# Layer 0 of a four-layer graph kernel: a whole last row tile, one broadcast on VectorE, later weight loads and a new order list

## The chip, the core and the metric

The kernel runs on one core of a Trainium2 chip. The metric is the device time of one execution in microseconds (us), the median of several runs. The core has five engines that the profile names PE (TensorE, the matrix engine; PEld is its weight load), DVE (VectorE), ACT (ScalarE), POOL (GpSimd) and SP (SyncE, which here only issues DMAs). Sixteen DMA engines move data between HBM and the on-chip memory.

## The reference

Node features `x` (2708 x 128) pass through four layers of message passing over a sparse weighted adjacency matrix `adj` (2708 x 2708, about 2.4% of it not zero). After each layer the result is added to `x` and normalized. Only layer 0 is touched by the change:

```
s = x @ msg_w[:, :128].T;  d = x @ msg_w[:, 128:].T
messages[i, j] = gelu(s[i] + d[j] + msg_b)          # 128 numbers for each pair
aggregated[i] = sum over j of adj[i, j] * messages[i, j]
h = gelu(concat(x, aggregated) @ upd_w.T + upd_b) + x
x = layernorm(x + layernorm(h))
...  # layers 1 to 3
```

## The kernel before

**Tiles.** A gelu for every pair would be 2708 x 2708 x 128 of them. The kernel uses that most pairs have weight zero. The rows i are cut into `LT` = 22 row tiles of `LR` = 125 rows, each in `NC` = 5 groups of `RG` = 25; the columns j into `NB` = 22 blocks of `JB` = 124. Within one block each row rarely has more than `CAP` = 5 neighbours. So each neighbour gets a rank within its block, and a slot (row, rank) in one of 5 x 25 partitions of a group. The matrices `S` (one-hot, 16-bit) pick for each slot the row of `d` and the weight; a product with `same` adds `s`.

**One block, on the engines.** PE `begin` (L1099) puts `s` into one of three PSUM slots `sl`; PE `pick` (L1107) adds the picked `d` and puts the weights beside it; ACT (L145) takes the gelu into one of six buffers `g`; DVE `weigh` (L1124) makes the small matrix `W`; PE `add_up` (L1115) multiplies `W` by `g` and sums into `acc`. After 22 blocks ACT copies `acc` out (L1120, `out`): that is the hand-over of a row tile. `turn` (L1049 to L1052) and `close` (L1056) turn the sum into a column range of `aggT`.

**What each row tile needs beforehand.** For each of three thirds of the columns: the load of `at` (L953, L956, the adjacency transposed, issued on SP), a `mask` on DVE (L879), ranks by a triangular matmul on PE (L886), a cast on ACT (L889), five `S` on DVE (L909), the weights in two 16-bit parts, `hi` on ACT (L902) and `lo` on DVE (L904). The untransposed rows `ar` come by six loads (L962). They serve the neighbours with a rank past `CAP`: DVE keeps their weights (`past`, L928), finds the largest (L936) and their columns (L982); POOL gathers the rows of `d` by index (L993) onto rows of `s` (started by a load on SP, L985); ACT and DVE weigh and sum them into `extra`. All this is done while the row tile before is in its blocks.

**The last row tile.** 21 x 125 = 2625, so 83 rows are left. Before, the last tile loads 83 rows and columns (`self.r = 83`), and DVE clears each `at` first (L877).

**The start.** `turn_x` transposes `x`; `prepare(n)`, n = 0 to 5, computes four blocks of `d` and four tiles of `s` and of `u` (the x part of the update), splits them into 16-bit `hi` and `lo` (ACT L831, DVE L840, L837), spreads `d` over the five groups (`spread_over`, on POOL, L798) and stores four tables to HBM from SP (L803, L806).

**The order.** The order of instructions on each engine is not written by hand. `Order.add` takes steps with an engine, an assumed cost, a due time (in units of blocks) and what they read and write; `Order.run` plays them through in Python at build time and emits them in the order in which they start. At each moment an engine takes the ready step with the smallest due time; PE adds `STAY` to the due time of a step that is of another kind than the one before:

```
s = min(can, key=lambda s: (s.due[0] + self.STAY * (s.kind != kinds.get(e, s.kind)), s.due[1]))
```

The kinds on PE are `"s"` (begin), `"all"` (pick, ranks, turn) and `"sums"` (add_up). The result is a fixed list; on the chip each engine goes through its own list in order and waits where data are not there yet.

**Weights of later layers.** `weight`, `column`, `across` and `side_by_side` load a weight at the first call. Before, the first calls are in layers 1 to 3, and the program's scheduler issues these DMAs early: they lie between 9 and 48 us in the profile.

Of the kernel before, what the change touches and what calls it, by code (L numbers as in the profile page):

```python
# [23 lines left out]
P = 128  # L24
# [56 lines left out]
class Order:  # L81
# [6 lines left out]

    LATENCY, TURN, STAY = 0.12, 0.1, 3.0

# [65 lines left out]
class Plan:  # L156
# [7 lines left out]
    LOAD, LATENCY = 1.28, 0.2  # L164
# [84 lines left out]
def gnn_stack(ctx: ExitStack, tc: tile.TileContext, t, out: bass.AP):  # L249
    nc = tc.nc  # L250
    N, D = t["x"].shape
# [69 lines left out]
    class Values:  # L321
# [33 lines left out]
        def add(self, a, b):  # L355
            return self.tt(a, b, ALU.add)
# [250 lines left out]
    NB = 22  # L607
# [21 lines left out]
    with ExitStack() as l0:  # L629
# [10 lines left out]
        with ExitStack() as msg:  # L640
# [79 lines left out]
            def columns_of(sl, a, b):  # L720
# [6 lines left out]
            order = Order()  # L727
            DUE = {"load": -69.5, "load_s": 34, "load_row": -9, "start_far": 204.5, "rank": -21, "rank_row": -18.5,
                   "begin": -0.8, "pick": -0.5, "add_up": 3.5, "turn": 34, "out": 41, "cast": -20, "a_hi": 7,
                   "gelu": -7.5, "far_weigh": 96, "close": 72.5, "far_gelu": 101.5, "weigh": -60.5, "largest": -8.5,  # L730
                   "index": 7.5, "mask": -12, "far_sum": -14.5, "past": -59.5, "max": -3, "a_lo": 1, "S": 1,
                   "fetch": 176}
            add = order.add
# [21 lines left out]
            def prepare(n):  # L755

                b0, b1 = 4 * n, min(4 * n + 4, NB)
                a0, a1 = 4 * n, min(4 * n + 4, NT)
                due = 4 * n - 40
                kd, ks = 2 * n % 3, (2 * n + 1) % 3  # L760
# [36 lines left out]
                def spread_over(v):  # L797
                    nc.gpsimd.tensor_copy(v[:, :, 1:, :], v[:, :, 0:1, :].to_broadcast([JB, b1 - b0, NC - 1, D]))  # L798

# [5 lines left out]
                def store(tab, v):  # L805
                    nc.sync.dma_start(out=tab[a0 * P:a1 * P, :].rearrange("(n p) d -> p n d", p=P), in_=v)  # L806
# [18 lines left out]
                if N < a1 * P:  # L825
# [16 lines left out]
                    reads=[("g", gd), ("hi", n)], writes=[("lo", n)])  # L842
                add("POOL", 2.2, lambda: spread_over(lo), due + 1, reads=[("lo", n)], writes=[("lo", n, 1)])
                add("SP", 0.1, lambda: store(s_tab, s), due + 1, reads=[("far", gf)], writes=[("s_tab", n)], lag=4.0)
                add("SP", 0.2, store_d, due + 1, reads=[("g", gd)], writes=[("d_tab", n)], lag=4.0)
                add("SP", 0.2, store_parts, due + 1, reads=[("parts", gf), ("parts", gf, 1), ("far", gf)],
                    writes=[("sq_tab", n)], lag=4.0)
                add("PE", 1.0, u_products, due + 12, reads=x_in, writes=["acc"], lag=0.2)
                add("DVE", 0.7, u_out, due + 12, reads=["acc"], writes=[("g", gu)])
                add("SP", 0.1, lambda: store(u_tab, u), due + 12, reads=[("g", gu)], writes=[("u_tab", n)], lag=4.0)  # L850

            class Rows:


                def __init__(self, t):
                    self.t, self.r0 = t, t * LR
                    self.r = min(P, N - self.r0)
                    self.pieces = range(self.r0 // BANK, min(self.r0 + P - 1, N - 1) // BANK + 1)
                    self.agg, self.s3, self.v = agg, s3_all[t % 2], v_all[:, t, :]
                    self.extra, self.cand = extra_all[t % 2], cand_all[t % 2]  # L860

                def add(self):
                    t = self.t
                    first = t * NB
                    add("SP", 0.4, self.load_s, first + DUE["load_s"], reads=[("sq_tab", n) for n in self.pieces],
                        writes=[("s3", t % 2)], lag=4.0)
                    for h, (b0, b1) in enumerate(thirds):
                        self.add_third(h, first + b0, b1 - b0)
                    self.add_far(first)

                def add_third(self, h, due, n):
# [7 lines left out]
                    add("DVE", 0.63 * share, lambda: nc.vector.tensor_scalar(  # L879
# [16 lines left out]
                    for k in range(2):  # L896
# [3 lines left out]
                    hi, lo = (v[:, b0:b1, :, D:] for v in dA)  # L900
                    source = at[:, :n, :LR].rearrange("p b (c i) -> p b c i", c=NC)
                    add("ACT", 0.97 * share, lambda: nc.scalar.activation(hi, source, AF.Copy, scale=A_SCALE), due + DUE["a_hi"],  # L902
# [3 lines left out]
                        reads=[k_at, ("a_hi", h)], writes=[("a_lo", h)])  # L906
                    ranks = rk[:, :n, :LR].rearrange("p b (c i) -> p b c i", c=NC)
                    for k in range(CAP):
# [4 lines left out]
                def add_rows(self, m, mask, k_mask, due):  # L913
# [5 lines left out]
                    one, share = ("misc", t, m, "rows"), n / PB  # L919
                    add("SP", 0.1, lambda: self.load_row(m, ar), due + DUE["load_row"], writes=[k_ar], lag=5.0)  # L920

# [18 lines left out]
                def load_s(self):  # L940
                    for q in range(2):
                        src = sq_tab[q, self.r0:self.r0 + LR, :].rearrange("(c i) d -> i c d", c=NC)
                        for k, (a, e) in enumerate(spans(0, NC, 3)):
                            p = k * HALF + q * RG
                            nc.sync.dma_start(out=self.s3[p:p + RG, :e - a, :D], in_=src[:, a:e, :])

                def load(self, h, at):
                    r0, r = self.r0, self.r
                    b0, b1 = thirds[h]
                    full = min(b1, NFB)  # L950
                    src = adjT[b0 * JB:full * JB, r0:r0 + r].rearrange("(b p) i -> p b i", p=JB)
                    for p0, p1 in even(JB):
                        nc.sync.dma_start(out=at[p0:p1, :full - b0, :r], in_=src[p0:p1])  # L953
                    if full < b1:
                        for p0, p1 in even(N - NFB * JB):
                            nc.sync.dma_start(out=at[p0:p1, full - b0, :r],  # L956
                                              in_=adjT[NFB * JB + p0:NFB * JB + p1, r0:r0 + r])

                def load_row(self, m, ar):
                    b1 = min((m + 1) * PB, NB)  # L960
                    n_in = min(b1 * JB, N) - m * PB * JB
                    nc.sync.dma_start(out=ar.rearrange("p b j -> p (b j)")[:self.r, :n_in],  # L962
                                      in_=adj[self.r0:self.r0 + self.r, m * PB * JB:m * PB * JB + n_in])

                def add_far(self, first):
# [11 lines left out]
                    for n in range(NOV):  # L977
# [6 lines left out]
                            reads=[("v", t, n), *o_keys], writes=[("ix", f)])  # L984
                        add("SP", 0.1, lambda far=far: nc.sync.dma_start(  # L985
                            out=far, in_=s_tab[self.r0:self.r0 + P, :][:, None, :].to_broadcast([P, 8, D])), due + DUE["start_far"],
# [52 lines left out]
                def add_turn(self, due):  # L1039
                    one = ("misc", self.t, "turn")  # L1040
                    add("PE", 0.85, self.turn, due + DUE["turn"], reads=[("extra", self.t % 2), "agg"], writes=[one],
                        lag=0.08, take="misc", kind="all")
                    add("ACT", 0.2, self.close, due + DUE["close"], reads=[one],
                        writes=[("xT", k) for k in range(len(spans(0, NT, 4)))], give=("misc", one, 1))
# [9 lines left out]
                def close(self):  # L1054
                    ps = misc.rearrange("p a b -> p (a b)")
                    nc.scalar.copy(aggT[:, self.r0:self.r0 + LR].rearrange("p (c i) -> p c i", c=NC),  # L1056
                                   ps[:, :32 * NC].rearrange("p (c i) -> p c i", c=NC)[:, :, :RG])
# [1045 lines left out]
```

## Time and profile before

| | us |
|---|---|
| median of 3 runs | 1827.45 (1826.45 to 1828.74) |
| the profiled execution | 1825.73 |
| its span, first to last instruction | 1824.0 |
| from the span's start to the first pick (L1107) | 62.9 |
| hand-over of row tile 0 | 101.8 |
| hand-over of row tile 21, the last | 800.3 |

| engine | busy us | share of the span |
|---|---|---|
| PE | 1548.3 | 85% |
| DVE | 1350.9 | 74% |
| ACT | 1070.6 | 59% |
| POOL | 595.0 | 33% |

In lines of the profile, the first number of a timeline row is the start from the span's beginning, the second the time it took; then follow engine (SPq is SP's queue, where the time is that of issuing), line, operation, and the output and input tiles with buffer numbers left out. A bracket tells how long the engine was idle before and what ended that. In rows of groups, the numbers behind the bar are the busy time, the mean time of one in ns, and the idle time before them. A row of waits gives engine, tile and line that waited, what it waited for, the sum, the number of times and the longest.

### The profile page before, as it was taken

What the parts mean: (1) busy time and instruction counts of PE and PEld (TensorE: products, weight loads), DVE (VectorE), ACT (ScalarE), POOL (GpSimd) and SP (SyncE); (2) the same over time, 40 slices, a digit from 0 to 9 for tenths busy, and PEclk for the clock granted to TensorE, in tenths of its full rate; (3) what the DMA queues carried; (4) which work ended last, traced back from release to release, by engine and by line L of the source; (5) the groups of instructions that cost most, each with busy time, mean ns of one, the idle gap of its engine ahead of it and who ended that gap; (6) DMA issues with size and microseconds to landing.
All of it is one profiled execution on the core that took longest, in us unless ns stands there. A gap on an engine that the chain in (4) does not pass through costs nothing.

```text
span 1824.0 us, 36369 instructions
## 1 busy us (share of the span) xinstructions
PE 1548.3 (85%) x14033; PEld 937.2 (51%) x14033; DVE 1350.9 (74%) x3129; ACT 1070.6 (59%) x1846; POOL 595.0 (33%) x389
## 2 busy tenths in 40 slices
PE   5799999999999999563999993678888895399995
PEld 4577777777777777452444442322222342144442
DVE  8799999999999999566788858658875873850004
ACT  3487787888878788453353434668877753421003
POOL 7287767677777776351000000000000000000000
PEclk8799999999999999886999996669987897599997
DMA  8677767667676765232244400314333555253431
GB/s 193 161 157 145 160 133 172 140 156 150 137 169 138 166 144 109 56 64 92 98 152 153 153 5 0 105 39 143 141 125 108 166 158 239 87 212 123 152 127 33
DMA packets 228558, 235.40 MB, mean 129 GB/s; under 512 B 28140, under 2 KB 213294, under 8 KB 221786
## 3 DMA queue, kind: packets, MB, share of 16 engines
q1 hardware_dynamic: 183670, 212.18, 37.3%
q0 software_dynamic: 44704, 20.80, 9.8%
q8 instruction: 112, 1.84, 0.4%
q14 instruction: 72, 0.59, 0.1%
HBM read 217.77 MB, written 15.15 MB: 128 GB/s over the span
## 4 chain that ended last, share of the span: by engine, by line
PE 38%; DVE 7%; ACT 6%; issue 1%; DMA 0%; SPq 0%; ACTq 0%; DVEq 0%
PE acc L2000 11%; PE lg L1388 6%; PE acc L1395 5%; PE accV L1728 5%; PE ps L1656 4%; PE accO L1732 2%; PE ps L1711 2%; DVE arena L1690 1%; ACT arena L1662 1%; PE ps L1657 1%; ACT arena L1683 1%; DVE arena L1714 1%; ACT x L455 1%; PE ps L523 1%; PE ps_w L1356 1%
## 5 line engine op out<-in xcount | busy, mean ns | idle before, releaser
L993 POOL DMA_INDIRECT far<-d_tab,ix x308 | 522.4, 1696 | 231.9 <-ACT agg L1120 50.0
L145 ACT ACTIVATE g<-sl 128x640 f32<-128x640 f32 x484 | 334.9, 708 | 150.4 <-PE sl L1107 102.9
L1107 PE MATMUL sl<-dA,S 124*128 124x153 f16 x4840 | 384.6, 232 | 1.3 <-DVE S L909 1.3
L1107 PEld LDWEIGHTS <-S 124*128 124x128 f16 x4840 | 326.4, 98 | 64.6 <-issue 59.6
L1099 PE MATMUL sl<-s,same 50*128 50x459 f16 (+1 forms) x968 | 145.6, 332 | 30.3 <-DVE W L1124 28.7
L1115 PE MATMUL acc<-g,W 128*32 128x128 f32 x4840 | 163.9, 277 | 0.1
L1124 DVE TENSOR_TENSOR W<-sl,own 128x125 f32<-128x125 f32 x484 | 129.0, 278 | 31.9 <-ACT g L145 31.4
L1389 ACT ACTIVATE w<-lg,row_L_gnn_gate_bias 128x512 f32<-128x512 f32 (+1 forms) x132 | 83.4, 636 | 108.2 <-PE lg L1388 107.0
L1115 PEld LDWEIGHTS acc<-g,W 128*32 128x32 f32 x4840 | 126.6, 110 | 22.0 <-issue 11.3
L1643 POOL TENSOR_TENSOR arena<-arena,off 128x128 f32<-128x128 f32 (+1 forms) x22 | 21.7, 986 | 351.5 <-DMA arena<-in_adjT 284.0
L909 DVE TENSOR_SCALAR S<-rk 124x1000 f16<-124x1000 bf16 (+1 forms) x330 | 124.5, 421 | 9.9 <-PE sl L1107 9.9
L982 DVE FIND_INDEX8 ix<-v,o 128x8 uint32<-128x2728 f32 x44 | 131.7, 2994 | 0.0
L1728 PE MATMUL accV<-arena,X 128*128 128x512 f32 (+4 forms) x264 | 124.8, 593 | 6.5 <-DVE arena L1694 6.5
L1388 PE MATMUL lg<-qT,mT 128*128 128x512 f32 (+2 forms) x264 | 121.2, 548 | 3.7 <-ACT w L1389 3.1
L1395 PE MATMUL acc<-w,both 128*128 128x512 f32 (+2 forms) x264 | 121.3, 547 | 0.0
L525 DVE TENSOR_TENSOR g<-ps,row_L_gnn_b 128x512 f32<-128x512 f32 (+2 forms) x14 | 7.9, 573 | 148.3 <-PE ps L523 148.3
L1656 PE MATMUL ps<-XT 128*128 128x512 f32 (+8 forms) x150 | 90.3, 691 | 32.1 <-ACT arena L1662 26.5
L2000 PE MATMUL acc<-at,x 128*128 128x512 f32 (+2 forms) x156 | 66.2, 575 | 48.5 <-ACT x L455 48.5
L1023 ACT ACTIVATE far<-far,v 128x128 f32<-128x128 f32 x308 | 105.2, 412 | 0.7
L1390 DVE TENSOR_TENSOR w<-w,at 128x512 f32<-128x512 f32 (+1 forms) x132 | 82.6, 626 | 27.1 <-ACT w L1389 27.0
L936 DVE MAX8 cand<-o 128x8 f32<-128x248 f32 x242 | 90.7, 406 | 0.0
L1099 PEld LDWEIGHTS <-same 50*128 50x128 f16 x968 | 43.6, 94 | 90.3 <-issue 68.0
(359 smaller groups left out, 2564.9 us busy)
## 6 DMA issues: line engine op xcount, KB each, us to landing
at<-in_adjT SPq DMA_DIRECT2D x42, 1354.0 KB
ar<-in_adj SPq DMA_DIRECT2D x105, 248.0 KB
far<-s_tab SPq DMA_DIRECT2D x44, 512.0 KB
at<-in_adjT SPq DMA_DIRECT2D x42, 448.0 KB
arena<-in_adjT SPq DMA_DIRECT2D x21, 704.0 KB
arena<-in_adjT SPq DMA_DIRECT2D x21, 650.0 KB
held<-in_adjT SPq DMA_DIRECT2D x7, 1354.0 KB
f_tab<-arena SPq DMA_DIRECT2D x10, 704.0 KB
```

Of the source, the lines that this page charges most:

```text
L145: s.emit()
L982: add("DVE", 3.0, lambda n=n, ix=ix: nc.vector.max_index(ix, v[:, n * 8:n * 8 + 8], o_all[:, :NB * JB]), due + DUE["index"], reads=[("v", ...
L993: nc.gpsimd.indirect_dma_start(out=far[:, k, :], out_offset=None, in_=d_tab[:, :], in_offset=bass.IndirectOffsetOnAxis(ap=ix[:, k:k + 1], ...
L1099: nc.tensor.matmul(columns_of(sl, 0, DA)[:, a:e, :], same[p], self.s3[p, :e - a, :], start=True, stop=False)
L1107: nc.tensor.matmul(columns_of(sl, 0, DA)[:, c, :], S_all[h][:, n, c, :], dA[q][:, b, c, :], start=False, stop=q == 1 and c in (2, NC - 1))
L1115: nc.tensor.matmul(acc_all[q:q + 32, k, :], W_all[W][:, c, :], g_all[g][:, c, :], start=b == 0 and k == 0, stop=ends)
L1124: nc.vector.tensor_tensor(W[:, :, :RG], columns_of(sl, D, DA), own[:, None, :].to_broadcast([P, NC, RG]), op=ALU.mult)
L1388: nc.tensor.matmul(lg, mT[:, j * P:j * P + r], qT[:, a:b], start=True, stop=True)
L1395: nc.tensor.matmul(acc[k], mrow[:rows[j], j, :], ws[j][:rows[j], a:b], start=j == 0, stop=j == NT - 1)
L1656: nc.tensor.matmul(ps, XT[:, self.js], XT[:, c], start=True, stop=False)
L1728: nc.tensor.matmul(Pair.acc[0][:, a:b], X[:self.r, self.j, :], self.w_[:, a:b], start=first, stop=last)
L2000: nc.tensor.matmul(acc[k], src[:rows[j], j, :], at[:rows[j], a:b], start=j == order[0], stop=j == order[-1])
```

## The change

- **The last row tile** is rows 2580 to 2707, whole 128 rows; its last 125 are used (`o = 3`, `used`). Rows 2583 to 2624 are computed a second time. The three clears of `at` go. The matrix `spread`, which puts `extra` in place in `turn`, is rewritten for the last tile by a DVE copy behind the turn of tile 20.
- **`spread_over`** runs on VectorE instead of GpSimd (twelve copies, all at the start).
- **Later layers' weights**: eleven steps load them from within layer 0's list, placed behind the first gather, with due times one row tile apart from the fifth on.
- **The list is redone**: `STAY` is 42 instead of 3, nearly all due times are new, and steps on SP have costs of 0.4 to 1.7 where they had 0.1 to 0.4.

```diff
-    LATENCY, TURN, STAY = 0.12, 0.1, 3.0
+    LATENCY, TURN, STAY = 0.12, 0.1, 42.0
...
-            DUE = {"load": -69.5, "load_s": 34, "load_row": -9, "start_far": 204.5, "rank": -21, "rank_row": -18.5,
-                   "begin": -0.8, "pick": -0.5, "add_up": 3.5, "turn": 34, "out": 41, "cast": -20, "a_hi": 7,
-                   "gelu": -7.5, "far_weigh": 96, "close": 72.5, "far_gelu": 101.5, "weigh": -60.5, "largest": -8.5,
-                   "index": 7.5, "mask": -12, "far_sum": -14.5, "past": -59.5, "max": -3, "a_lo": 1, "S": 1,
-                   "fetch": 176}
+            DUE = {"piece": 0, "spread": -10, "s_out": 23.5, "d_out": 37, "u": 25, "load": -125, "load_s": 94.5,
+                   "load_row": -58.5, "start_far": 206, "rank": -20, "rank_row": -18.5, "begin": -1.8, "pick": 0.5,
+                   "add_up": 3, "turn": 34.5, "out": 57.5, "cast": -58.5, "a_hi": 21, "gelu": -9.5, "far_weigh": 97.5,
+                   "close": 113.5, "far_gelu": 106, "weigh": -63.5, "largest": -8.5, "index": -35, "mask": -10,
+                   "far_sum": -34, "past": -77, "max": -4.5, "a_lo": -12, "S": 4, "fetch": 211}
...
-                    nc.gpsimd.tensor_copy(v[:, :, 1:, :], v[:, :, 0:1, :].to_broadcast([JB, b1 - b0, NC - 1, D]))
+                    nc.vector.tensor_copy(v[:, :, 1:, :], v[:, :, 0:1, :].to_broadcast([JB, b1 - b0, NC - 1, D]))
...
-                add("POOL", 2.2, lambda: spread_over(hi), due, reads=[("hi", n)], writes=[("hi", n, 1)])
+                add("DVE", 0.65, lambda: spread_over(hi), due + DUE["spread"], reads=[("hi", n)], writes=[("hi", n, 1)])
...
-                add("SP", 0.1, lambda: store(s_tab, s), due + 1, reads=[("far", gf)], writes=[("s_tab", n)], lag=4.0)
-                add("SP", 0.2, store_d, due + 1, reads=[("g", gd)], writes=[("d_tab", n)], lag=4.0)
+                add("SP", 0.45, lambda: store(s_tab, s), due + DUE["s_out"], reads=[("far", gf)], writes=[("s_tab", n)], lag=4.0)
+                add("SP", 0.9, store_d, due + DUE["d_out"], reads=[("g", gd)], writes=[("d_tab", n)], lag=4.0)
...
-                add("PE", 1.0, u_products, due + 12, reads=x_in, writes=["acc"], lag=0.2)
+                add("PE", 1.0, u_products, due + DUE["u"], reads=x_in, writes=["acc"], lag=0.2)
...
-                    self.t, self.r0 = t, t * LR
-                    self.r = min(P, N - self.r0)
+                    self.t, self.r0 = t, min(t * LR, N - P)
+                    self.o = P - LR if t == LT - 1 else 0
+                    self.used = slice(self.o, self.o + LR)
...
-                    if self.r < P:
-                        add("DVE", 0.9, lambda: nc.vector.memset(at, 0.0), due + DUE["load"], writes=[k_at])
-                    add("SP", 0.2, lambda: self.load(h, at), due + DUE["load"], writes=[k_at], lag=7.0)
+                    add("SP", 0.8, lambda: self.load(h, at), due + DUE["load"], writes=[k_at], lag=7.0)
...
-                nc.sync.dma_start(out=ar.rearrange("p b j -> p (b j)")[:self.r, :n_in],
-                                  in_=adj[self.r0:self.r0 + self.r, m * PB * JB:m * PB * JB + n_in])
+                nc.sync.dma_start(out=ar.rearrange("p b j -> p (b j)")[:, :n_in],
+                                  in_=adj[self.r0:self.r0 + P, m * PB * JB:m * PB * JB + n_in])
...
+            for n, (engine, load) in enumerate((
+                    ("SP", side_by_side), ("SP", lambda: weight("L1_gnn_W_q")), ("SP", lambda: weight("L1_gnn_W_k")),
+                    ("SP", lambda: weight("L1_gnn_W_upd", P)), ("SP", lambda: column("L1_gnn_b_msg")),
+                    ("SP", lambda: weight("L3_gnn_W")), ("POOL", lambda: across("L1_gnn_gate_bias")),
+                    ("POOL", lambda: across("L1_gnn_ln_gamma")), ("POOL", lambda: across("L1_gnn_ln_beta")),
+                    ("POOL", lambda: across("L2_gnn_att_b")), ("POOL", lambda: across("L3_gnn_b")))):
+                add(engine, 0.55, load, (5 + n) * NB, reads=[("far", 0, 0)])
...
+            add("DVE", 0.2, lambda: nc.vector.tensor_copy(
+                spread[:, :, :RG], ident[:, R[-1].used].rearrange("p (c i) -> p c i", c=NC)), (LT - 1) * NB + 10,
+                writes=["spread"])
```

More of the change, by code (lines that the diff above doesn't have):

```diff
@@ L758, in prepare @@
                 a0, a1 = 4 * n, min(4 * n + 4, NT)
-                due = 4 * n - 40
+                due = 4 * n - 40 + DUE["piece"]
                 kd, ks = 2 * n % 3, (2 * n + 1) % 3
@@ L842, in prepare @@
                     reads=[("g", gd), ("hi", n)], writes=[("lo", n)])
-                add("POOL", 2.2, lambda: spread_over(lo), due + 1, reads=[("lo", n)], writes=[("lo", n, 1)])
-                add("SP", 0.1, lambda: store(s_tab, s), due + 1, reads=[("far", gf)], writes=[("s_tab", n)], lag=4.0)
-                add("SP", 0.2, store_d, due + 1, reads=[("g", gd)], writes=[("d_tab", n)], lag=4.0)
-                add("SP", 0.2, store_parts, due + 1, reads=[("parts", gf), ("parts", gf, 1), ("far", gf)],
+                add("DVE", 0.65, lambda: spread_over(lo), due + 1 + DUE["spread"], reads=[("lo", n)], writes=[("lo", n, 1)])
+                add("SP", 0.45, lambda: store(s_tab, s), due + DUE["s_out"], reads=[("far", gf)], writes=[("s_tab", n)], lag=4.0)
+                add("SP", 0.9, store_d, due + DUE["d_out"], reads=[("g", gd)], writes=[("d_tab", n)], lag=4.0)
+                add("SP", 0.9, store_parts, due + 1, reads=[("parts", gf), ("parts", gf, 1), ("far", gf)],
                     writes=[("sq_tab", n)], lag=4.0)
-                add("PE", 1.0, u_products, due + 12, reads=x_in, writes=["acc"], lag=0.2)
-                add("DVE", 0.7, u_out, due + 12, reads=["acc"], writes=[("g", gu)])
-                add("SP", 0.1, lambda: store(u_tab, u), due + 12, reads=[("g", gu)], writes=[("u_tab", n)], lag=4.0)
+                add("PE", 1.0, u_products, due + DUE["u"], reads=x_in, writes=["acc"], lag=0.2)
+                add("DVE", 0.7, u_out, due + DUE["u"], reads=["acc"], writes=[("g", gu)])
+                add("SP", 0.45, lambda: store(u_tab, u), due + DUE["u"], reads=[("g", gu)], writes=[("u_tab", n)], lag=4.0)
             class Rows:
                 def __init__(self, t):
-                    self.t, self.r0 = t, t * LR
-                    self.r = min(P, N - self.r0)
+                    self.t, self.r0 = t, min(t * LR, N - P)
+                    self.o = P - LR if t == LT - 1 else 0
+                    self.used = slice(self.o, self.o + LR)
                     self.pieces = range(self.r0 // BANK, min(self.r0 + P - 1, N - 1) // BANK + 1)
@@ L864, in add @@
                     first = t * NB
-                    add("SP", 0.4, self.load_s, first + DUE["load_s"], reads=[("sq_tab", n) for n in self.pieces],
+                    add("SP", 1.7, self.load_s, first + DUE["load_s"], reads=[("sq_tab", n) for n in self.pieces],
                         writes=[("s3", t % 2)], lag=4.0)
@@ L900, in add_third @@
                     hi, lo = (v[:, b0:b1, :, D:] for v in dA)
-                    source = at[:, :n, :LR].rearrange("p b (c i) -> p b c i", c=NC)
+                    source = at[:, :n, self.used].rearrange("p b (c i) -> p b c i", c=NC)
                     add("ACT", 0.97 * share, lambda: nc.scalar.activation(hi, source, AF.Copy, scale=A_SCALE), due + DUE["a_hi"],
@@ L906, in add_third @@
                         reads=[k_at, ("a_hi", h)], writes=[("a_lo", h)])
-                    ranks = rk[:, :n, :LR].rearrange("p b (c i) -> p b c i", c=NC)
+                    ranks = rk[:, :n, self.used].rearrange("p b (c i) -> p b c i", c=NC)
                     for k in range(CAP):
@@ L919, in add_rows @@
                     one, share = ("misc", t, m, "rows"), n / PB
-                    add("SP", 0.1, lambda: self.load_row(m, ar), due + DUE["load_row"], writes=[k_ar], lag=5.0)
+                    add("SP", 0.4, lambda: self.load_row(m, ar), due + DUE["load_row"], writes=[k_ar], lag=5.0)
                     def rank():
@@ L941, in load_s @@
                     for q in range(2):
-                        src = sq_tab[q, self.r0:self.r0 + LR, :].rearrange("(c i) d -> i c d", c=NC)
+                        src = sq_tab[q, self.r0 + self.o:self.r0 + self.o + LR, :].rearrange("(c i) d -> i c d", c=NC)
                         for k, (a, e) in enumerate(spans(0, NC, 3)):
@@ L947, in load @@
                 def load(self, h, at):
-                    r0, r = self.r0, self.r
+                    r0, r = self.r0, P
                     b0, b1 = thirds[h]
@@ L984, in add_far @@
                             reads=[("v", t, n), *o_keys], writes=[("ix", f)])
-                        add("SP", 0.1, lambda far=far: nc.sync.dma_start(
+                        add("SP", 0.45, lambda far=far: nc.sync.dma_start(
                             out=far, in_=s_tab[self.r0:self.r0 + P, :][:, None, :].to_broadcast([P, 8, D])), due + DUE["start_far"],
@@ L1040, in add_turn @@
                     one = ("misc", self.t, "turn")
-                    add("PE", 0.85, self.turn, due + DUE["turn"], reads=[("extra", self.t % 2), "agg"], writes=[one],
+                    add("PE", 0.85, self.turn, due + DUE["turn"], reads=[("extra", self.t % 2), "agg", "spread"], writes=[one],
                         lag=0.08, take="misc", kind="all")
@@ L1055, in close @@
                     ps = misc.rearrange("p a b -> p (a b)")
-                    nc.scalar.copy(aggT[:, self.r0:self.r0 + LR].rearrange("p (c i) -> p c i", c=NC),
+                    nc.scalar.copy(aggT[:, self.r0 + self.o:self.r0 + self.o + LR].rearrange("p (c i) -> p c i", c=NC),
                                    ps[:, :32 * NC].rearrange("p (c i) -> p c i", c=NC)[:, :, :RG])
```

## The prediction

> **What bounds the kernel now.** I read the busy slices of the page first, then the times at which each row tile of layer 0 hands over its sum (ACT, L1120), then the windows around whatever breaks the rhythm, and in those the timeline, the waits and the DMA answer. Times are microseconds.
>
> ```profile
> PE   5799999999999999563999993678888895399995
> PEclk8799999999999999886999996669987897599997
> ```
>
> A slice is 45.6 us. PE is near full in slices 3 to 16, and there are two weak places in the part that the change touches: the start (slices 1 and 2) and slices 17 and 18.
>
> ```profile
> 687.14 0.19 ACT L1120 ACTIVATION_READ_ACCUMULATOR agg<-acc 128x1 f32 x1
> 719.43 0.19 ACT L1120 ACTIVATION_READ_ACCUMULATOR agg<-acc 128x1 f32 x1
> 771.88 0.20 ACT L1120 ACTIVATION_READ_ACCUMULATOR agg<-acc 128x1 f32 x1
> 800.34 0.19 ACT L1120 ACTIVATION_READ_ACCUMULATOR agg<-acc 128x1 f32 x1
> ```
>
> Tile 0 hands over at 101.8, and from tile 5 on the distance is 32.33 each time (687.14 to 719.43 is one). Tile 20 takes 52.45. So 52.45 - 32.33 = 20.1 us are lost once, in tile 20, which is when tile 21, the last, is fetched and ranked ahead.
>
> ```profile
> 101.80:739.30 637.50, 626.51 (x10140) 484.74 (x10138) 602.08 (x1526) 514.47 (x1025) 470.62 (x276) 1.00 0.69 147
> 739.30:756.00 16.70, 0.12 (x2) 0.10 (x1) 0.94 (x3) 1.45 (x2) 7.01 (x5) 0.64 0.33 77
> ```
>
> The columns are the stretch, its length, busy PE, PEld, DVE, ACT and POOL, the granted clock, the DMA share and GB/s. In the loop PE is 98% busy and DVE 94%. From 739.3 to 756.0 all of them stand.
>
> ```profile
> 731.48 8.76 SPq L985 DMA_DIRECT2D far<-s_tab  x1
> 740.35 3.19 SPq L962 DMA_DIRECT2D ar<-in_adj  x1
> 743.62 4.36 SPq L953 DMA_DIRECT2D at<-in_adjT  x2
> ...
> 755.07 0.56 DVE L879 TENSOR_SCALAR mask<-at 124x768 bf16<-124x768 f32 x1 [17.05 <-DMA at<-in_adjT]
> ...
> 755.88 0.54 PE L1099 MATMUL sl<-s,same 50*128 50x459 f16 x2 [16.61 <-DVE W L1124]
> ```
>
> DVE waits 17.05 us for the last third of the last tile's `at`; `weigh` is behind it on DVE, and PE waits for `weigh`. That load was issued only at 743.6, because SP sat 8.76 us in one issue and 3.19 in the next, where such an issue takes 0.33 to 1.5 in the tile before. The DMA answer for 732 to 752 says why:
>
> ```profile
> GB/s 148 302 326 292 124 150 38 20 19 24 59 125 36 24 28 24 19 44 269 355 335 93 20 22 19 20 19 19 32 180 206 24 28 61 88 28 66 70 61 41
> ...
> ar<-in_adj SPq DMA_DIRECT2D x1, 160.8 KB
> ```
>
> For long stretches only 19 to 24 GB/s move, while loads of 128 rows reach 250 to 330. 160.8 KB are 83 rows of 1984 B; there the busy share of the 16 DMA engines is under a tenth, which is about one engine's pace. The last tile's six `ar` loads are five of 160.8 KB and one of 73.9 KB, together 0.90 MB; at 20 GB/s that is 45 us, more than the 32.3 us of a tile, and SP's later loads queue behind them.
>
> **The change, part by part.** The sum is made against the profiled execution, 1825.73 us (span 1824.0); the median, 1827.45, is 1.7 above it.
>
> *Last tile of 128 rows: -19.5 us.* The `ar` loads become the shape of all other tiles (248 and 114 KB), which never held the rhythm up. The three memsets of `at` (0.91 us of DVE each, each with a load behind it) go. If tile 20 keeps the rhythm, 20.1 us are saved; if only the standstill goes and not the ramp after it, 16.6 (the clock is 0.50 from 745 to 760). What would be late next is the copy that rewrites `spread` for the last tile: some 0.28 us of DVE (the same copy took that at 12.67), waiting for tile 20's turn. The late turn steps lie behind the last tile's blocks, so I charge 0 to 1 us. I take 19.5; bounds 16 to 20.1. The work itself is not shorter: 22 tiles as before.
>
> *Spread on VectorE, and the new order at the start: -12 us.*
>
> ```profile
> L840 DVE SCALAR_TENSOR_TENSOR dA<-g,dA 124x512 f16<-124x512 f32 x5 | 8.5, 1705 | 0.0
> L837 DVE SCALAR_TENSOR_TENSOR far<-far 128x512 f16<-128x512 f32 x5 | 7.8, 1565 | 0.0
> ...
> L909 DVE TENSOR_SCALAR S<-rk 124x1000 f16<-124x1000 bf16 x5 | 2.0, 423 | 0.0
> ```
> ```profile
> L798 POOL COPY dA<-dA 124x2048 f16<-124x2048 f16 x10 | 21.9, 2215 | 7.9 <-ACT dA L831 6.1 <-DVE dA L840 1.8
> ```
> ```profile
> 39.03 0.68 DVE L837 SCALAR_TENSOR_TENSOR far<-far 128x512 f16<-128x512 f32 x1
> ```
> ```profile
> DVE g L774 <- DMA u_tab<-g: 7.7, 1, 7.7
> ```
>
> The first product of the blocks (L1107) starts at 62.93. Until 47.7 DVE bounds the start (31.1 of 31.3 us busy from 16.4), and its operations are slow while POOL copies: 1.6 to 1.7 us against 0.68 at 39.03, when POOL copied nothing. Excess: L840 8.5 - 5 x 0.68 = 5.1, L837 7.8 - 3.4 = 4.4, the narrow L840 2.2 - 0.4 = 1.8, the two wide masks 3.1 - 1.4 = 1.7, the first L904 3.0 - 1.2 = 1.8: 14.8 us. Without POOL's copies that falls away, and twelve copies come onto DVE. Their price is not in the trace. Nearest is L909, sixteen-bit to sixteen-bit: 0.42 for 1000 elements, of which some 0.15 is fixed (the smallest DVE operations), so 0.15 + 2.05 x 0.27 = 0.70 for 2048; the other end is the pace of L837, 0.53 per 512, or 2.3. I take 0.75, nearer in type, and half for the two narrow ones: 10 x 0.75 + 2 x 0.45 = 8.4 (bound 25). DVE gains 14.8 - 8.4 = 6.4, or loses 10 at the far end.
>
> [...]
>
> Then DVE stands 7.7 us at a clear of `g`, for a `u_tab` store that SP issued only at 51.40, behind a `far` start and others; PE's products and the `S` steps wait behind it. The new list puts the `u` steps later (due +25 for +12), stores `s_tab` and `d_tab` later, counts 0.45 to 1.7 per SP step instead of 0.1 to 0.4, and takes seven weight loads of 0.4 to 0.7 us (3.6 us) off SP at the start. I count on most of this wait, 5.5 us. 6.4 + 5.5 = 12. The list may also delay a load that the first rank needs, so bounds are 4 us lost and 20 gained.
>
> *The weights: 0.* Eleven steps, seven DMAs on SP and seven on POOL at 0.55 us, spread over tiles 5 to 15. POOL is idle 26% in the loop (430 of 584 busy) and a gather that is late by 0.55 us has buffers ahead; if that cover were gone, 3.9 us. They read nothing that holds SP's queue, and layer 1 comes long after.
>
> *The list in the loop: -6 us.* STAY 42 makes PE stay with one kind of matmul while any is ready.
>
> ```profile
> PEld L1107 <- issue: 46.5, 181, 0.4
> PEld L1099 <- issue: 41.0, 159, 1.1
> ...
> PEld L886 <- issue: 7.4, 28, 0.4
> ```
> ```profile
> PE sl L1099 <- DVE W L1124: 7.8, 18, 1.1
> ```
>
> Over 135.3 to 719.4 (18 tiles), the weight loads pause 0.26 us at each change of kind, over 20 times a tile, some 5 us a tile; part of that is the drain of wide matmuls and stays. The ceiling is DVE: 551.3 of 584.1 us busy, so at most 1.8 us a tile, 1.3 if DVE keeps a little slack. The floor for the gain is none: three slots and six `g` buffers force much of the alternation whatever STAY says. And holding can cost: one more wait for a slot is 0.43 us (7.8 / 18), so two a tile lose 0.9. I take -0.3 a tile x 20 tiles = -6; bounds -26 and +18.
>
> Sum: -19.5 - 12 + 0 - 6 = -37.5; 1825.7 - 37.5 = 1788.2, and with the 1.7 between the profiled run and the median, 1790.
>
> **The rivals.** (1) Only the last tile's stall goes; DVE's new copies and another late store eat the gain at the start, and the loop stays at 32.33. For it: DVE is 99% busy there, so a copy of 2.3 us would undo all. 1825.7 - 19.5 + 1.7 = 1808. (2) Slower: in the loop PE holds one kind until no slot is free, then waits for gelu (0.71) and `weigh` (0.28) to free one. The waits of that kind are 18 in 18 tiles now, up to 1.1 us each. It decides once the loop loses (19.5 + 12) / 20 = 1.6 us a tile, some two waits of 0.9 more; at three (2.7 us a tile) it is 1827.45 - 31.5 + 54 = 1850. Against it: PE takes whatever kind is ready, and waits only where none is. (3) The stall stays: the last tile's late load is SP's order and not the row count, so the redone list only shifts it. 1825.7 - 18 + 1.7 = 1809. Against it: 20 GB/s fits one 83-row DMA at a time, and no 128-row tile shows it.
>
> **How the numbers follow.** The forecast as a whole gets 0.70, rival 1 0.18, rival 2 with a loop that eats everything 0.06, rival 3 0.03; the remaining 0.03 is a loop better than my bound. The range takes the forecast's ends: -20 - 20 - 20 gives 1767, and -17 - 3 + 5 gives 1812, which includes rivals 1 and 3. About 0.2% (3.7 us) is what a measurement tells from no change: faster 0.92, same 0.02, slower 0.06.
>
> **What would show it.** Right: no standstill above 2 us between the last two handovers, `ar` loads all of 248 or 114 KB, tile 20 at the common distance; L837 and L840 at 0.68, spread at 0.7 to 0.8 on DVE, L1107 starting near 50, tile 0 handing over near 90; a common distance of 31 to 32.3 with DVE at 95% or more. Wrong: a distance above 33, many waits of PE for `weigh`, a first L1107 after 60, or a time above 1812 or below 1767.

## The result, and the profile after

| | before | after |
|---|---|---|
| median, us | 1828.1 (6 runs, 1818.75 to 1830.82) | 1807.74 (6 runs, 1795.35 to 1811.34) |
| the profiled execution | 1825.73 | 1797.42 |
| first pick (L1107 before, L1106 after) | 62.96 | 66.08 |
| row tile 0 hands over | 101.78 | 105.13 |
| row tile 1 hands over | 135.32 | 140.97 |
| mean distance, tiles 2 to 19 | 32.45 | 32.34 |
| tile 20 / tile 21 takes | 52.45 / 28.46 | 32.41 / 27.01 |
| last hand-over of layer 0 | 800.34 | 782.48 |
| from there to the end of the span | 1023.7 | 1013.1 |

The ratio is 0.9879, 95% interval [0.9838, 0.9920]: faster by 1.2%. The busy slices of the page of the changed kernel, 44.9 us each (line numbers behind `spread_over` are one or so lower than before):

```profile
PE   5799999999999999954999993678887994499995
...
PEclk8799999999999999976999996679998996599998
```

The hole in slices 17 and 18 is gone (the weak slices that are left are the change of layers), the weak start is not. The same two things in the handovers of the last four tiles, from ACT's timeline:

```profile
690.77 0.20 ACT L1119 ACTIVATION_READ_ACCUMULATOR agg<-acc 128x1 f32 x1
...
723.06 0.20 ACT L1119 ACTIVATION_READ_ACCUMULATOR agg<-acc 128x1 f32 x1
...
755.47 0.20 ACT L1119 ACTIVATION_READ_ACCUMULATOR agg<-acc 128x1 f32 x1
...
782.48 0.19 ACT L1119 ACTIVATION_READ_ACCUMULATOR agg<-acc 128x1 f32 x1
```

Tile 20 takes 755.47 - 723.06 = 32.41, like its neighbours. Of the 28.4 us between the two spans, the start loses 5.65, tiles 2 to 19 give 2.0, tile 20 gives 20.0, tile 21 gives 1.45: layer 0 is 17.9 shorter. The other 10.5 lie behind layer 0, where the change edits nothing. The windows of 290 us that begin 370 us after the last hand-over of layer 0, first before, then after (columns as in the prediction):

```profile
1170.30:1460.30 290.00, 242.36 (x702) 84.49 (x703) 210.40 (x188) 220.48 (x233) 18.43 (x18) 0.83 0.37 126
```
```profile
1152.50:1442.50 290.00, 241.74 (x748) 85.30 (x748) 218.03 (x200) 227.69 (x242) 19.24 (x17) 0.87 0.39 133
```

The granted clock is 0.83 against 0.87, and 748 matmuls get done instead of 702. This is no work of the change, for over the thirteen profiles of this study the part behind layer 0 takes 1011.9 to 1015.2 in five (clock 0.87 to 0.88 in such a window) and 1023.2 to 1026.4 in eight (0.82 to 0.83), and the changed kernel itself has 1013.1, 1023.9 and 1023.2. So I compare handovers in layer 0 first, and medians second.

**Where the start went.** The first pick of the changed kernel:

```profile
66.08 3.46 PE L1106 MATMUL sl<-dA,S 124*128 124x153 f16 x30 [1.91 <-DVE S L908]
```

SP's timeline of the changed kernel, then of the kernel before:

```profile
15.72 4.03 SPq L961 DMA_DIRECT2D ar<-in_adj  x3
19.80 0.73 SPq L289 DMA_DIRECT2D w_both<-in_L_gnn_W_msg  x1
23.15 0.33 SPq L289 DMA_DIRECT2D w_both<-in_L_gnn_W_upd  x1
23.52 1.29 SPq L267 DMA_DIRECT2D w_L_gnn_W_q<-in_L_gnn_W_q  x1
...
26.34 0.87 SPq L803 DMA_DIRECT2D d_tab<-g  x2
...
50.10 0.36 SPq L984 DMA_DIRECT2D far<-s_tab  x1
...
51.64 0.55 SPq L806 DMA_DIRECT2D u_tab<-g  x1
54.21 0.36 SPq L984 DMA_DIRECT2D far<-s_tab  x1
```
```profile
19.42 1.19 SPq L803 DMA_DIRECT2D d_tab<-g  x2
...
38.73 0.52 SPq L267 DMA_DIRECT2D w_L_gnn_W_q<-in_L_gnn_W_q  x1
```

The weight loads did not move back but ahead: six of the seven on SP now stand before the first store of `d_tab`, which is issued at 26.34 instead of 19.42. (The last rows show `u_tab` stores in turn with `far` starts; that comes up in the experiments.) What the loads do is in the waits of 16.4 to 66 of the changed kernel:

```profile
DVE g L820 <- DMA u_tab<-g: 7.8, 2, 4.2
PE sl L783 <- ACT g L787: 7.6, 2, 6.9
DVE dA L798 <- ACT dA L831: 4.8, 1, 4.8
ACT g L787 <- DMA d_tab<-g: 4.3, 1, 4.3
...
DVE g L774 <- DMA u_tab<-g: 2.1, 1, 2.1
```

Read from the fourth row up: ACT may not overwrite the buffer `g` until the late store has read it (4.3); PE's products for the next piece wait for ACT (6.9 in one); DVE waits for the `d` of that piece (4.8). Later DVE stands three times before a buffer `g` that a `u_tab` store still reads (7.8 + 2.1 = 9.9; it was 7.7, once). The DVE work itself did get shorter, as the groups between 10 and 70 show:

```profile
L798 DVE COPY dA<-dA 124x2048 f16<-124x2048 f16 x10 | 6.9, 700 | 5.1 <-ACT dA L831 4.8
...
L840 DVE SCALAR_TENSOR_TENSOR dA<-g,dA 124x512 f16<-124x512 f32 x5 | 3.4, 687 | 0.0
...
L837 DVE SCALAR_TENSOR_TENSOR far<-far 128x512 f16<-128x512 f32 x5 | 3.4, 674 | 0.0
```

DVE is busy 22.8 us of the 31.3 between 16.4 and 47.7, where it was 31.1 (third of the busy times, first before, then after):

```profile
16.40:47.70 31.30, 19.15 (x120) 16.30 (x119) 31.09 (x31) 12.81 (x23) 26.09 (x16) 0.83 0.84 205
```
```profile
16.40:47.70 31.30, 18.96 (x106) 15.32 (x106) 22.81 (x40) 12.75 (x22) 0.00 (x0) 0.68 0.82 193
```

The time saved became waiting.

The cause of the early loads is in the list. The section on the change calls them placed behind the first gather; they are not. `Order.add` lets a step wait for the last writer of what it reads, among the steps added so far. The weight steps are added ahead of the row tiles, so `("far", 0, 0)` has no writer yet. They wait for nothing, SP is idle for a moment in the plan, and their due times only rank them among ready steps.

### The profile page after: what moved, and what is told of

Read it like the earlier page. It is cut to its first block, busy times and chain, and to the rows that moved or that the text cites. A ratio compares the mean times of both kernels' runs of the same rounds, so it can differ in the third digit from the quotient of the medians.

```text
span 1795.6 us, 36325 instructions
## 1 busy us (share of the span) xinstructions
PE 1531.0 (85%) x14033; PEld 936.3 (52%) x14033; DVE 1342.2 (75%) x3139; ACT 1069.3 (60%) x1846; POOL 566.1 (32%) x377
## 4 chain that ended last, share of the span: by engine, by line
PE 38%; DVE 7%; ACT 7%; issue 1%; ACTq 0%; DVEq 0%
PE acc L2009 11%; PE lg L1397 6%; PE acc L1404 6%; PE accV L1737 5%; PE ps L1665 3%; PE accO L1741 2%; PE ps L1720 1%; ACT arena L1671 1%; PE ps L1666 1%; DVE arena L1699 1%; ACT arena L1692 1%; DVE arena L1723 1%; ACT x L455 1%; PE ps L523 1%; PE ps_w L1365 1%
## 5 line engine op out<-in xcount | busy, mean ns | idle before, releaser
L992 POOL DMA_INDIRECT far<-d_tab,ix x308 | 517.1, 1679 | 251.1 <-ACT g L145 157.0
L1106 PE MATMUL sl<-dA,S 124*128 124x153 f16 x4840 | 378.8, 232 | 1.9 <-DVE S L908 1.9
L1106 PEld LDWEIGHTS <-S 124*128 124x128 f16 x4840 | 329.6, 98 | 47.2 <-issue 39.9
L1665 PE MATMUL ps<-XT 128*128 128x512 f32 (+8 forms) x150 | 84.1, 647 | 32.2 <-ACT arena L1671 26.5
L927 DVE SCALAR_TENSOR_TENSOR o<-misc,ar 128x496 f32<-128x496 f32 x132 | 82.6, 626 | 28.0 <-PE misc L923 13.0
L888 ACT CAST rk<-misc 124x512 bf16<-124x512 f32 x132 | 72.2, 547 | 44.8 <-PE misc L885 44.2
```

The source lines that it names most:

```text
L992: nc.gpsimd.indirect_dma_start(out=far[:, k, :], out_offset=None, in_=d_tab[:, :], in_offset=bass.IndirectOffsetOnAxis(ap=ix[:, k:k + 1], ...
L1106: nc.tensor.matmul(columns_of(sl, 0, DA)[:, c, :], S_all[h][:, n, c, :], dA[q][:, b, c, :], start=False, stop=q == 1 and c in (2, NC - 1))
L1665: nc.tensor.matmul(ps, XT[:, self.js], XT[:, c], start=True, stop=False)
```

## The experiments

My theory after this result: the last tile's step is right and is one DMA's shape; the start is lost to two placements on SP (weight loads, then `far` starts ahead of the `u_tab` stores); the copies on DVE are worth what was predicted. Rivals: the start is DVE's own, or the list's as a whole; the last tile's gain is the list's. All handovers:

| run | first pick | tile 0 | tile 1 | mean 2 to 19 | tile 20 | tile 21 | layer 0 ends | median, us | ratio to before |
|---|---|---|---|---|---|---|---|---|---|
| even83 | 61.02 | 99.12 | 133.03 | 32.47 | 33.62 | 28.33 | 779.35 | 1806.01 | 0.9922 [0.9893, 0.9950] |
| whole_only | 63.95 | 102.43 | 136.38 | 32.49 | 32.96 | 29.07 | 783.27 | 1801.56 | 0.9887 [0.9831, 0.9942] |
| weights_behind | 58.29 | 97.02 | 131.81 | 32.02 | 32.50 | 27.22 | 767.89 | 1795.15 | 0.9848 [0.9794, 0.9902] |
| weights_and_far | 51.05 | 89.72 | 124.51 | 32.01 | 32.48 | 27.21 | 760.41 | 1789.81 | 0.9840 [0.9794, 0.9887] |
| changed_again | 65.59 | 105.86 | 140.09 | 32.41 | 32.57 | 27.01 | 783.05 | 1801.54 | 0.9870 [0.9821, 0.9920] |
| spread_on_pool | 56.94 | 94.48 | 128.82 | 32.45 | 32.55 | 27.21 | 772.70 | 1795.39 | 0.9847 [0.9783, 0.9911] |
| spread_only | 61.91 | 100.25 | 136.49 | 33.44 | 55.11 | 30.10 | 823.54 | 1842.07 | 1.0103 [1.0041, 1.0165] |
| stay3 | 51.01 | 90.75 | 123.73 | 34.35 | 34.53 | 30.64 | 807.22 | 1831.35 | 1.0034 [1.0005, 1.0062] |
| weights_and_far_again | 51.38 | 90.40 | 125.38 | 32.02 | 32.49 | 27.21 | 761.41 | 1776.06 | 0.9772 [0.9734, 0.9810] |
| weights_in_tiles | 49.98 | 86.97 | 121.77 | 32.03 | 32.48 | 27.22 | 757.99 | 1783.25 | 0.9794 [0.9760, 0.9827] |
| changed_third | 66.73 | 106.30 | 141.10 | 32.08 | 32.35 | 27.00 | 777.81 | 1797.03 | 0.9862 [0.9827, 0.9898] |

The first four ran on one chip, the next four on a second, the last three on a third. The kernel before had 1816.91, 1827.27 and 1823.27 there.

### The stall of the last tile: its cause, and its share

**even83**: the kernel before, and only the six `ar` loads of the last tile cut in two.

```diff
-                    nc.sync.dma_start(out=ar.rearrange("p b j -> p (b j)")[:self.r, :n_in],
-                                      in_=adj[self.r0:self.r0 + self.r, m * PB * JB:m * PB * JB + n_in])
+                    for p0, p1 in even(self.r):       # 83 rows: 80 and 3
+                        nc.sync.dma_start(out=ar.rearrange("p b j -> p (b j)")[p0:p1, :n_in],
+                                          in_=adj[self.r0 + p0:self.r0 + p1, m * PB * JB:m * PB * JB + n_in])
```

> The kernel before with one edit: the last tile's row loads keep their 83 rows but are issued as two DMAs, of 80 and 3 rows, in the way the at loads already are. Order list, clears of at and 83-row at loads stay. If the standstill comes from 83 rows that one DMA engine must carry alone, tile 20 hands over 32 to 34 us after tile 19 instead of 52.45 and layer 0 ends about 18 to 20 us earlier (total near 1808). If it comes from the clears of at or from the order on SP, tile 20 stays above 45 us.

The DMA issues of this run between 690 and 760, two rows of SP, and its last three handovers:

```profile
ar<-in_adj SPq DMA_DIRECT2D x5, 155.0 KB
...
ar<-in_adj SPq DMA_DIRECT2D x5, 5.8 KB
```
```profile
724.67 2.04 SPq L986 DMA_DIRECT2D far<-s_tab  x2
...
728.05 1.64 SPq L953 DMA_DIRECT2D at<-in_adjT  x2
```
```profile
717.40 0.20 ACT L1121 ACTIVATION_READ_ACCUMULATOR agg<-acc 128x1 f32 x1
...
751.02 0.20 ACT L1121 ACTIVATION_READ_ACCUMULATOR agg<-acc 128x1 f32 x1
...
779.35 0.19 ACT L1121 ACTIVATION_READ_ACCUMULATOR agg<-acc 128x1 f32 x1
```

The same bytes in the same order, 80 rows and 3 in place of 83, and tile 20 takes 33.62 instead of 52.45: 18.8 of its 20.1 us of loss are gone, with the clears, the 83-row `at` and SP's order left in place. The two `far` starts take SP 2.04 us where they took 13.54, and the load of `at` behind them is issued at 728.05 instead of 743.62. So the shape of the DMA is the cause, and rival 3 of the prediction (SP's order) falls.

The packets of 1984 bytes in the traces show what differs: in the kernel before, between 716 and 756, they go one after the other (of 28.1 us with such a packet under way, two overlap for 0.9, and never three), at a median of 0.081 us each. In the changed kernel, whose `ar` loads all have 128 rows, two or more overlap for 4.6 of 5.8 us between 720 and 760, at the same median. Why 83 rows go so and 128, or 80 and 3, do not, no run shows.

**whole_only**: the kernel before with the whole last tile (rows 2580 on, no clears, the rewritten `spread`) and nothing else of the change.

```diff
-                    self.t, self.r0 = t, t * LR
-                    self.r = min(P, N - self.r0)
+                    self.t, self.r0 = t, min(t * LR, N - P)
+                    self.o = P - LR if t == LT - 1 else 0
+                    self.used = slice(self.o, self.o + LR)
...
```

> The kernel before with only the whole last tile (128 rows, no clears, spread rewritten); old list, spread on GpSimd, weights as before. If the changed kernel's gain is the last tile alone, tile 20 takes 32.3 to 32.6, tile 1 still hands over at 135.3, the last tile near 780: 20 us less than before, and 2 us less at the end of layer 0 than the changed kernel, because the start is as before. If the new list has a part in the gain, the last two tiles are longer than the changed kernel's 32.41 and 27.01.

The last two tiles take 32.96 and 29.07, together 2.6 more than in the changed kernel, so that much there is the new list's. Layer 0 ends at 783.27; the changed kernel ends it at 782.48, 783.05 and 777.81. Rival 1's reading of the sum holds: what the change brought is the last tile, and all its other parts together gave between nothing and 5.5 us. By tile 1 they lose 3.7 to 4.7, and the tiles behind it win that back.

The start itself scatters between executions. The kernel before, even83 and whole_only have the same list on every engine up to tile 1, and hand tile 1 over at 135.32, 133.03 and 136.38, with first picks at 62.96, 61.02 and 63.95. A difference of some 3 us there says nothing by itself.

### The start: two placements on SP

**weights_behind**: the changed kernel, with the eleven weight steps added behind all row tiles. They now have the last writer of `("far", 0, 0)` to wait for, not the first gather as I expected, and are issued at 748 to 754.

```diff
             R = [Rows(i) for i in range(LT)]
             for row in R:
                 row.add()
...
+            for n, (engine, load) in enumerate((     # was ahead of R
                     ("SP", side_by_side), ("SP", lambda: weight("L1_gnn_W_q")), ("SP", lambda: weight("L1_gnn_W_k")),
...
```

> The changed kernel with the weight steps added to the list behind the row tiles' steps, so that what they read is the first gather (in the changed kernel nothing has written it when they are added, and seven of them stand on SP at 19.8 to 28.3 us). If those loads hold the start up, PE's gap at 22.8 to 29.7 us shrinks below 2 us and tile 1 hands over 4 to 6 us earlier than 140.97. If the start is held by the u stores alone, the gap only moves and tile 1 stays within 1.5 us of 140.97.

**weights_and_far**: that, and the first two tiles' `far` starts (L984) listed behind the `u_tab` stores.

```diff
-                            reads=[("s_tab", k) for k in self.pieces],
+                            reads=[("s_tab", k) for k in self.pieces] + [("u_tab", k) for k in range(6 if t < 2 else 0)],
```

> As the one before, and the first three far loads stand behind the six u_tab stores on SP. If DVE's waits for u_tab (4.2, 3.6 and 2.1 us in the changed kernel) come from u stores that queue behind far loads, they fall to under 4 us together, the first L1106 starts near 54 to 58 instead of 66.05, and tile 1 hands over 8 to 12 us before 140.97. If they come from the stores' own landing, tile 1 is as with the weights moved alone, within 1.5 us.

The waits of 16.4 to 66 of weights_behind, then of weights_and_far:

```profile
DVE g L820 <- DMA u_tab<-g: 7.5, 2, 3.9
...
PE sl L783 <- ACT g L787: 1.8, 2, 1.1
...
DVE g L774 <- DMA u_tab<-g: 1.6, 1, 1.6
```
```profile
PE sl L783 <- ACT g L787: 1.8, 2, 1.2
...
DVE g L774 <- DMA u_tab<-g: 1.8, 1, 1.8
```

Without the early loads PE waits 1.8 for ACT instead of 7.6, and the first pick comes 7.8 earlier; DVE's wait for `u_tab` stays at 9.1 (7.5 + 1.6). Without the `far` starts ahead of the stores (SP waits 5.1 us at them in the changed kernel and 5.0 in weights_behind, for `sq_tab` stores to land) that wait falls to 1.8, and the first pick comes another 7.2 earlier:

```profile
51.05 3.86 PE L1106 MATMUL sl<-dA,S 124*128 124x153 f16 x30 [1.02 <-DVE S L908]
```

That is the "near 50" of the prediction. Both are placements on SP, neither is DVE's work. Three executions of the changed kernel have the first pick at 65.59 to 66.73, three with the start of weights_and_far at 49.98 to 51.38, so both steps are clear of the scatter.

**spread_on_pool**: weights_and_far with the copies back on GpSimd at their old cost, to price that step alone.

```diff
-                    nc.vector.tensor_copy(v[:, :, 1:, :], v[:, :, 0:1, :].to_broadcast([JB, b1 - b0, NC - 1, D]))
+                    nc.gpsimd.tensor_copy(v[:, :, 1:, :], v[:, :, 0:1, :].to_broadcast([JB, b1 - b0, NC - 1, D]))
...
```

> The version with weights and far loads moved, and the twelve copies of d back on GpSimd at their old cost of 2.2. If the slowing of DVE by GpSimd's copies is what the move saves, L837 and L840 are at 1.5 us or more again and the first L1106 starts 4 to 8 us later than 51.0. If the start is held by other things, DVE is slow again but the first L1106 is within 1.5 us of 51.0.

The groups of the start of this run:

```profile
L840 DVE SCALAR_TENSOR_TENSOR dA<-g,dA 124x512 f16<-124x512 f32 x5 | 8.8, 1767 | 0.0
...
L837 DVE SCALAR_TENSOR_TENSOR far<-far 128x512 f16<-128x512 f32 x5 | 8.4, 1684 | 0.0
```

1767 and 1684 ns, where the same lines take 687 and 674 in the changed kernel; the first pick comes at 56.94, 5.9 later (5.6 to 7.0 against the three executions with the copies on DVE). The prediction said 6.4.

**spread_only**: the kernel before with only the copies on DVE.

```diff
-                add("POOL", 2.2, lambda: spread_over(hi), due, reads=[("hi", n)], writes=[("hi", n, 1)])
+                add("DVE", 0.65, lambda: spread_over(hi), due - 10, reads=[("hi", n)], writes=[("hi", n, 1)])
...
```

> The kernel before with only the twelve copies on VectorE (due 10 earlier, cost 0.65, the rest of the list's numbers as before). By the prediction's step the start saves some 6 us of DVE: first L1107 near 57 instead of 62.93. If DVE then only waits longer for the u_tab store (7.7 us before), the wait grows and the first L1107 stays within 2 us of 62.93.

Its waits of 16.4 to 66:

```profile
DVE g L774 <- DMA sq_tab<-far: 9.4, 1, 9.4
...
DVE g L774 <- DMA d_tab<-g: 4.8, 1, 4.8
```

The first pick comes 1.0 earlier, at 61.91, which is inside the 61.02 to 63.95 of the old list in three executions, and the kernel is slower by 1.0%. The same copies that are worth 5.9 with the stores in good order give nothing that can be told from scatter without: DVE waits 14.2 for two stores instead. And since the planner deals the whole list anew from the changed costs, the loop went to 33.44 a tile. So this run shows what the copies do at the start; its total is another list's.

### The loop

**stay3**: weights_and_far with STAY back at 3.

```diff
-    LATENCY, TURN, STAY = 0.12, 0.1, 42.0
+    LATENCY, TURN, STAY = 0.12, 0.1, 3.0
```

> The version with weights and far loads moved, and STAY back at 3; all due times as changed. If holding one kind of matmul makes the loop faster, the common distance rises from 32.03 towards the 32.33 of the kernel before. If the due times do it, it stays within 0.1 of 32.03. If holding was harmful, it falls below 31.9.

The waits between 140 and 700, in stay3 and then in weights_and_far:

```profile
PEld L1098 <- issue: 61.3, 186, 1.4
...
PEld L1106 <- issue: 38.3, 170, 0.4
...
PE sl L1098 <- DVE W L1123: 24.0, 32, 1.4
PEld acc L1114 <- issue: 18.9, 81, 0.4
```
```profile
PEld L1098 <- issue: 38.1, 140, 0.7
PEld L1106 <- issue: 30.9, 123, 0.4
...
PE sl L1098 <- DVE W L1123: 8.0, 17, 0.5
PEld acc L1114 <- issue: 6.8, 35, 0.2
```

With the new due times, STAY 3 costs 34.35 a tile and STAY 42 32.01. PE changes kind more often, and waits for `weigh` 32 times, not 17, at up to 1.4. But against the old pair of STAY and due times (32.33 when in rhythm) the new pair gains only 0.3 a tile: `STAY` and the due times belong together, and neither alone says what the list is worth. (The old due times with STAY 42 were not run.)

**changed_again** and **changed_third**: the changed kernel once more, on the second and the third chip.

> The changed kernel itself, on the same chip as the three others of this call. In its first profile the tiles of the loop scatter from 32.03 to 32.75 (mean 32.34 over tiles 2 to 19), while the version with the weights behind has the same lists on PE, DVE and ACT and runs at 32.02. If the weights' place also disturbs the loop, this run's mean is again 32.3 or more; if the scatter belonged to that one run, it is near 32.02. Tile 1 should hand over near 141 again, the layer end near 782 or, with a quiet loop, 776.

> The changed kernel once more, beside the two others on the same chip: first pick near 65.8, row tile 0 at 105 to 106, layer 0 ending at 782 to 783, a median of 1800 to 1809. If its layer 0 ends where it ended twice before while the total differs from 1797 or 1807 of those profiles, the remaining difference is outside layer 0.

The start repeats (first pick 65.6 and 66.7, tile 1 at 140.1 and 141.1). The loop does not: tiles 3 to 19 take 32.03 to 32.99 in the first two profiles of this kernel, and a regular 32.03 with one outlier of 33.00 in the third. I had taken the scatter to belong to its list; the third profile shows that the list alone does not make it. What sets it off is not settled: the chip is not ruled out, for spread_on_pool scatters too (32.02 to 32.78 from tile 3 on) and ran on the second chip like changed_again, while weights_behind and weights_and_far run regularly on the first and weights_and_far_again on the third.

**weights_in_tiles**: weights_and_far, with each weight load put by hand into the emission of a step of row tiles 5 to 15. The lists of PE, DVE and ACT stay as they are.

```diff
+                    b1 = on_sp[self.t - 5]() if m == 0 and 5 <= self.t < 11 else 0; ...
...
+                                on_pool[t - 11]() if k == 0 and 11 <= t < 16 else 0; nc.gpsimd.indirect_dma_start(
```

> weights_and_far with the later layers' weight loads put inside the loop: each SP load is issued right ahead of the first ar load of row tiles 5 to 10, and each POOL load right ahead of the first gather of each half of row tiles 11 to 15 (the two bias halves go with row tile 5's). The lists of PE, DVE and ACT are the same. The prediction's step (weights cost nothing inside the tiles, at most 3.9 if the cover were gone): distances stay at 32.03 in all tiles, the handover of the last tile within 1 us of 760.4, the median equal to that of weights_and_far_again. Rival (a load on SP or POOL inside the loop is felt): the tiles with a load take 0.3 to 0.6 longer each, layer 0 ends 3 to 6 later.

Two of the loads, with their time in ns and their start:

```profile
L267 SPq DMA_DIRECT2D w_L_gnn_W_q<-in_L_gnn_W_q x1: 1548/1548/1548, 203.5 to 203.5; - x1
```
```profile
L280 POOL DMA_DIRECT2D row_L_gnn_ln_gamma<-in_L_gnn_ln_gamma x1: 1228/1228/1228, 436.9 to 436.9; - x1
```

They take up to 1.55 us on SP and 1.24 on POOL, two to three times what I had assumed, and still cost nothing in the loop: from tile 1 to tile 20 it is 609.0 us, against 608.8 in weights_and_far_again. Its tile 0 came 3.4 earlier with the same list up to there, about the scatter of the old list's start. Its median is 7.2 above that of weights_and_far_again, where I had expected none. In the two profiled executions that lies behind layer 0 (1023.4 against 1014.1, with clocks of 0.83 and 0.87), so the medians cannot price the loads.

**weights_and_far_again**: weights_and_far, beside the changed kernel.

> The version of weights_and_far again, unchanged, beside the changed kernel on one chip. My theory (the start of the changed kernel was lost to two placements on SP's queue, and the rest of the change works): first pick near 51.0, row tile 0 handing over near 89.7, layer 0 ending near 760, 22 before the changed kernel. Then its median lies about 20 below that of the changed kernel and some 35 to 40 below the kernel before (ratio 0.978 to 0.985). Rival (the difference to the changed kernel seen so far, 1790 against 1802 to 1808, was mostly the clock of layer 2): the handovers repeat, but the medians differ by less than 8. A regular distance of 32.03 in the loop would show that it belongs to this list; a scatter of 32.0 to 32.8, that it is chance of one execution.

On the same chip the medians are 1776.06 and 1797.03, 21.0 apart; layer 0 ends 16.4 earlier, not 22, because the loop of the changed kernel ran regularly in this profile. This version beats both kernels: 2.3% under before, where the change gives 1.4% there (1.6% on the first chip). By its handovers it reached the start and the loop that the prediction counted on: 800.34 - 761.41 = 38.9 us less in layer 0, where the sum was 37.5.

## Why the prediction was right or wrong

- **Forecast against measurement.** 1790 was predicted, 1807.74 measured: 17.7 too low. The start was to give 12 and took 5.65: 17.65. The other deviations nearly cancel in the median: the loop fell 4.0 short, tiles 20 and 21 gave 2.0 more than the sum had, and the medians lie 2.5 further apart than layer 0 explains. The time is that of rival 1 (1808), which is partly luck: the start was not at nothing but at a loss, and those other terms made up for it. Of its mechanism half is right: another late store ate the gain, the copies on DVE did not. The range (1767 to 1812) was narrower than the prediction's own bounds for its terms, which reach from 1761 to 1833.
- **Last tile, -19.5: right.** -20.0 in the handovers, and the cause as argued: the row loads of 83 rows, one at a time and one packet after the other, shown by even83 and by the packets of the kernel before. That the pace is one engine's was my estimate, from a DMA share under a tenth of 16 engines; no run shows which engines carry them. In the standstill not all engines stood, as the prediction says: its row has POOL busy for 7.0 us. The late rewriting of `spread` took 0.28, at 766.4, and nothing waited for it.
- **Spread on VectorE, 6.4 of the 12: right as a price, wrong as a gain.** The copies took 0.70 and 0.43 (0.75 and 0.45 assumed), L837 and L840 fell to 0.67 and 0.69, and with the stores in order the step is worth 5.9; alone, in the old list, it shows no gain. In the changed kernel DVE stopped being the bound. I had costed DVE's list and not asked which store is late next.
- **The `u_tab` wait, 5.5 of the 12: the step that failed.** The new list was to shorten the wait, partly since it "takes seven weight loads of 0.4 to 0.7 us (3.6 us) off SP at the start" (by the rows before, their issues add up to 3.45). Six of them were put earlier instead, ahead of the first `d_tab` store, and that costs 7.8 of the first pick, through PE's wait for ACT. The wait for `u_tab` itself grew from 7.7 to 9.9; it shrinks, to 1.8, only with the `far` starts behind the stores, which the change does not do, and that is worth another 7.2. The mistake with the loads is in reading the list: I took a due time for a start time and a read for a dependence, without looking for a writer among the steps added before. My text named a delayed load as the bound (4 us lost); it came to 5.65. The sign of being wrong that it named, a first pick after 60, came at 66.08.
- **Weights in the loop, 0: right, but not what the change did.** Only weights_in_tiles puts them there.
- **The list in the loop, -6: right in size, not steady.** -0.30 a tile where the rhythm holds (32.33 to 32.03), -0.11 in the profiled execution, hence -2.0. Tile 21 gave another 1.45 that the sum did not have.
- **Rival 2** (PE holds a kind and starves): no sign. `weigh` keeps PE waiting 8.5 us in 140 to 700, 18 times; it was 6.7 there, 17 times (7.8 and 18 in the prediction's longer window).

## What to carry to other kernels

The transfers of 83 rows did not only take longer (19 to 24 GB/s): they held the queue that issued them (13.54 us for two starts behind 83-row loads, 2.04 behind split ones), and what then stood was a load far behind them. Splitting them (80 + 3) gave back 18.8 of the 20.1 us, so try that before changing the tiling for its sake. In a list made by a planner, a due time orders ready steps and delays none, so look up what each new step really waits for, and count it on every queue at the moment where it becomes ready. Here time taken off the busiest engine of the start was a gain only up to the next store in the queue: follow that store before booking it.

## What was not expected of the hardware

- In one and the same stage behind layer 0 the granted clock was 0.82 in one execution of weights_and_far and 0.87 in another, and the part behind layer 0 took 1026.4 and 1014.1 us. What sets the clock there is not known; it makes 10 us of a profiled pair's difference noise.
- The loop of one and the same list ran at a regular 32.03 a tile with one outlier in one execution, and between 32.03 and 32.99 in others.
- The load of a weight kept SP for 0.42 to 1.55 us in the loop, and that of a row spread over all partitions kept POOL for 0.53 to 0.75 at the start and 1.23 to 1.24 in the loop.
